# Keys, values, queries and energy of a one-core transformer block: four tiles from float32 operands, products paired on column halves

## The chip, the core and the metric

The kernel runs on one core of a Trainium2 chip. A core has a matrix engine (TensorE, PE in the profile, with its weight loads shown apart as PEld), VectorE (DVE), ScalarE (ACT), GpSimd (POOL) and SyncE (SP), each with its own instruction stream, and 16 DMA engines that move data between the chip's memory and the core's on-chip memory (SBUF). PE multiplies a stationary operand (the weights, up to 128 columns) with a moving operand and writes into eight accumulation banks (PSUM), which ACT and DVE read. The metric is the device time of one execution in microseconds (us).

## The reference

One attention layer without softmax, then a gated feed-forward network, each with a residual and a layer norm, for 4096 tokens of width 256. Cut to what matters here:

```python
Q = jnp.einsum('bne,de->bnd', x, wq)            # D = 64
K = jnp.einsum('bne,de->bnd', x, wk)
V = jnp.einsum('bne,de->bnd', x, wv)
energy = jnp.einsum('bnd,bne->bde', K, V)       # 64 x 64, over all tokens
context = jnp.einsum('bnd,bde->bne', Q, energy) * math.sqrt(3.0 / D)
out = jnp.einsum('bnd,ed->bne', context, wo)
x = _layernorm(x + out)
h = silu(x @ w1.T * w1_s) * (x @ w2.T * w2_s)   # 1024 wide, weights -1, 0, 1
h = gelu(h @ h1.T * h1_s)
h = gelu(h @ h2.T * h2_s)
x = _layernorm(x + h @ w3.T * w3_s)
```

All inputs and the output are float32.

## The kernel before

The tokens form eight tiles of 512 (T). A tile of the input comes in twice: transposed (`xt[t]`, 128 partitions x 2 x 512, for the attention's products) and as tokens (`x`, for the residual). Every engine runs its instructions in the order in which the program lists them; what one engine needs of another is kept by semaphores.

A product of float32 operands takes two records of load and multiply in the profile. The other way used here is the type float32r, in which a product is one record; an operand that it would round is split into two parts first: `hi`, the rounded value, cast by ACT, and `lo`, the rest, subtracted by DVE. Two products, with hi and with lo, are then added up.

**Attention, the stretch that the change touches (lines 421 to 694).** The transfers are listed on SP: `wkv` (keys' and values' weights), then `xt[0]` in two halves of its tokens, `xt[1]`, `wq1` (queries' weights, 64 columns), then `xt[2]` to `xt[7]` (lines 432 to 440); behind them blocks of a later layer's weights and `x`. On POOL: `wo`, `w1`, `w2` (from line 513), each after named transfers.

- `WARM` = 7 products of constants run on PE before any data is there (line 533).
- Tiles 0 to 2 (`WHOLE = 3`): `keys_values(t)` multiplies float32 tokens with `wkv`, 8 products of 128 columns into one bank, and ACT copies them to `kv[t]` (line 565).
- Tiles 3 to 7: `with_queries(t)` uses the two parts of the tokens (from `halves(t)`, lines 606 to 616) with the 192 columns `wvkq` of values, keys and queries: 16 products (line 578), two banks of two blocks of 128 tokens. ACT and DVE copy keys and values (lines 584 and 590), and the queries are split into hi and lo side by side in `stk[t]` (lines 585 and 586). `halves` is called two tiles ahead.
- Queries of tiles 0 to 2: `queries(t)`, four products of 512 columns with `wq`, in which the 64 columns stand twice (line 629); `stack(t)` makes the upper 64 partitions of `stk[t]` the rounded queries and the lower 64 the rest (lines 636 and 637).
- Queries of tiles 3 to 7 stand by tokens and are turned by PE: `turn_queries(t)`, four transposes (line 596), and `put_queries(t)`, a copy on ACT (line 600).
- `energy(t)` adds four products of 64 x 64 per tile to one 64-partition accumulator `pe` (line 619). ACT scales it into `es`, twice (line 663), one product with `wo` gives a 128 x 256 matrix (line 666), which ACT and DVE split into `m2hi` and `m2lo` (lines 667 and 668).
- `attention_out(t)` multiplies the stacked queries with both (lines 139 and 140). `attend_norm` adds the residual and normalizes on DVE, with a power on POOL (line 88).
- The first tile is turned (line 200), split (lines 208 and 209), and the feed-forward products begin: line 710 for the first half tile, then line 700.

`early` are sums of weight blocks on DVE for the later square layers (line 307 through `sums`), stored by POOL; `acc()` gives the six banks in turn.

**Behind it (from line 722)**: four passes of two tiles each through gate products (line 700), two square layers with seven block products each (line 295) and the last layer (line 855). In gaps of DVE, `check_job` compares weights with the rounded copies in use, piece by piece (23 pieces from `checks`, line 801); `inexact` holds the same for `wkv` (line 449). If anything differs, a general path runs afterwards.

The order of the main part, line 646 onwards:

```python
    for t in range(NT):
        if t < WHOLE:
            keys_values(t)
            continue
        if t + 2 < NT:
            halves(t + 2)
        elif t == NT - 1:
            early[0]()
        with_queries(t)
    queries(0)
    stack(0)
    halves(1)
    early[1]()
```

Of the kernel before, what the change touches and what calls it, by code (L numbers as in the profile page):

```python
# [32 lines left out]
KH = H // P  # L33
HK = KH // 2
EPS = 1e-5
WARM = 7
CSCALE = math.sqrt(3.0 / D)
SPREAD = 2.0**5
S1, S2, S3, S4, A11, A12, A22 = range(7)
# [5 lines left out]
def block_kernel(ctx: ExitStack, tc: tile.TileContext, a: dict, out: bass.AP):  # L45
# [19 lines left out]
    def const(name, shape, dt=F32):  # L65
        return cp.tile(shape, dt, tag=name, name=name)
# [9 lines left out]
    ones = const("ones", [P, 1])  # L76
    row = const("row", [1, P])
    eps = const("eps", [P, 1])
    inexact = const("inexact", [P, 1])
    m2hi = const("m2hi", [P, E], FR)  # L80
    m2lo = const("m2lo", [P, E], FR)
    flag = const("flag", [1, 1], I32)
# [23 lines left out]
    def weight(name, shape):  # L106
        return wp.tile(shape, FR, tag=name, name=name)
# [1 line left out]
    w1 = weight("w1", [P, KE, H])  # L109
    w2 = weight("w2", [P, KE, H])  # L110
    w3 = weight("w3", [P, KH, E])
    wq = weight("wq", [P, KE, P])
    stacks = weight("stk", [P, NT, T])
    stk = [stacks[:, t, :] for t in range(NT)]

# [17 lines left out]
    def attention_out(t):  # L133
        ps = []
        for g in range(NS // 2):
            po = aux[g].rearrange("p (j e) -> p j e", j=2)
            for j in range(2):
                q = stk[t][:, (2 * g + j) * P : (2 * g + j + 1) * P]
                nc.tensor.matmul(po[:, j, :], q, m2hi, start=True, stop=False)  # L139
                nc.tensor.matmul(po[:, j, :], q, m2lo, start=False, stop=True)  # L140
            ps.append(po)
        return ps

# [302 lines left out]

    nc.scalar.activation(once, mhalf[:, :1], AF.Silu)
    nc.scalar.copy(wvkq[:, :, : 2 * D], wkv)
    nc.vector.scalar_tensor_tensor(
        xT[:, 0, :, : 2 * D], wkv, 0.0, wvkq[:, :, : 2 * D].bitcast(F32),  # L450
        ALU.add, ALU.not_equal, accum_out=inexact,
    )

    def raw_blocks(layer, k, raw, queue=nc.sync):
        w = a[f"h{layer + 1}"]
# [67 lines left out]
    after(raw_blocks(0, 2, raws[2])[0], "w2")  # L523


    turn_of_acc = [5]

    def acc():
        turn_of_acc[0] += 1
        return bank[(turn_of_acc[0] - 1) % 6]  # L530
# [22 lines left out]
    def keys_values(t):  # L553
        x = xt[t]
        pk = acc().rearrange("p (s c) -> p s c", s=NS)
        for s in range(NS):
            for k in range(KE):
                nc.tensor.matmul(
                    pk[:, s, :], x[:, k, s * P : (s + 1) * P], wkv[:, k, :],
                    start=(k == 0), stop=(k == KE - 1),  # L560
                )
        kv_place(t)
        for i in ((0,), (2,), (3, 4))[t]:
            halves(i)
        nc.scalar.copy(kv[t], pk)

    def with_queries(t):

        kv_place(t)

        q = stk[t].rearrange("p (s i d) -> p s i d", s=NS, i=2)
        for g in range(2):
            ps = acc()[:, : 2 * V].rearrange("p (s c) -> p s c", s=2)
            for j in range(2):
                s = 2 * g + j
                for i, part in enumerate((xh[t], xl[t])):
                    for k in range(KE):
                        nc.tensor.matmul(  # L578
                            ps[:, j, :], part[:, k, s * P : (s + 1) * P], wvkq[:, k, :],
                            start=(i == 0 and k == 0), stop=(i == 1 and k == KE - 1),  # L580
                        )
# [23 lines left out]

    def halves(t):

        xh[t], xl[t] = places[t if t < 6 else t - 3]
        n = 2 if t in (WHOLE, WHOLE + 1) else 1
        for h in range(n):  # L610
            c = slice(h * T // n, (h + 1) * T // n)
            nc.scalar.copy(xh[t][:, :, c], xt[t][:, :, c])
            nc.vector.tensor_tensor(
                xl[t][:, :, c], xt[t][:, :, c], xh[t][:, :, c].bitcast(F32), ALU.subtract
            )

    def energy(t):
        for s in range(NS):
            nc.tensor.matmul(  # L619
                pe[:D], kv[t][:, s, :D], kv[t][:, s, D:P],  # L620
                start=(t == 0 and s == 0), stop=(t == NT - 1 and s == NS - 1),
            )

    def queries(t, ks=range(KE)):
        if t not in pq:
            pq[t] = acc()
        for k in ks:
            for i, part in enumerate((xh[t], xl[t])):
                nc.tensor.matmul(  # L629
                    pq[t], wq[:, k, :], part[:, k, :],  # L630
                    start=(k == 0 and i == 0), stop=(k == KE - 1 and i == 1),
                )

    def stack(t):

        nc.scalar.copy(stk[t], pq[t])
        nc.vector.tensor_tensor(  # L637
            stk[t][D:P], pq[t][D:P], stk[t][D:P].bitcast(F32), ALU.subtract
        )


    WHOLE = 3
    early = [*sums(0, 0, raws[0]), *sums(0, 1, raws[1])]
    for w in (wvkq[:, :, 2 * D :], wq[:, :, :D], wq[:, :, D:]):
        nc.vector.tensor_copy(w, wq1)
# [20 lines left out]
    nc.tensor.matmul(pm, es.rearrange("e c d -> e (c d)"), wo, start=True, stop=True)  # L666
    nc.scalar.copy(m2hi, pm)
    nc.vector.tensor_tensor(m2lo, pm, m2hi.bitcast(F32), ALU.subtract)
# [21 lines left out]
    split(0, 2)  # L690
    norm(2)
    norm(3)
    stack(1)
    stack(2)


    def gate_products(ps, w, o, slot, j, c=slice(0, T)):
# [87 lines left out]
    def second_sums(k):  # L785
# [167 lines left out]
    def bounds(step):  # L953

        if step == 0:
            nc.vector.tensor_reduce(some, mvo[:, : (NT - 2) * NS, 1], AX.X, ALU.max)
        if step == 1:
            nc.tensor.transpose(aux[0][:1, :P], some, ident)
            nc.vector.tensor_reduce(most[:1, 3:4], aux[0][:1, :P], AX.X, ALU.max)
        if step == 2:  # L960
            nc.tensor.matmul(aux[1][:, :1], row, most[:1, 3:4], start=True, stop=True)
            nc.vector.tensor_scalar(low, aux[1][:, :1], 1.0 / SPREAD, None, ALU.mult)
            nc.vector.tensor_scalar(high, aux[1][:, :1], SPREAD, None, ALU.mult)
        if step == 3:
            assert next_check.done == len(pieces) and not staged
            nc.vector.tensor_reduce(some, differ, AX.X, ALU.add)
            plus(some, some, inexact)
# [400 lines left out]
```

## Time and profile before

| what | value |
| --- | --- |
| median of 3 runs | 638.01 us (637.96 to 638.14) |
| the profiled execution's own time | 638.17 us |
| its span, first to last instruction | 636.4 us |
| last product of tiles 3 to 7 (L578) ends, queries of tile 0 (L629) begin | 22.11 us |
| energy (L619) begins | 23.15 us |
| first residual add (L160) begins | 29.94 us |
| first feed-forward product (L710) begins | 34.28 us |
| DMA rate 4.71 to 8.13 us, 8.13 to 12.39 us | 294 GB/s, 404 GB/s |
| landing of tiles 1, 2, 3, 4 of xt | 8.09, 10.26, 11.55, 12.83 us |

The profile is one execution. "Busy" is the time in which an engine has an instruction in flight; products on PE overlap, so the pace is read from start to start. An entry such as "[0.31 <-DMA f<-in_xt]" is idle time of the engine just before, and what ended it. In the view of waits the columns are: total us, times, longest us.

### The profile page before, as it was taken

The page shows a single profiled execution, that of the slowest core. Times are in us where ns is not written, and L with a number is a line of the kernel's source. Part 1 is how long each engine was busy: PE and PEld are TensorE (multiplying, and loading weights), DVE is VectorE, ACT ScalarE, POOL GpSimd, SP SyncE. Part 2 cuts the span into 40 slices and gives each one's busy share as a digit, 9 for nine tenths or more (in the row PEclk, how much of TensorE's full clock was granted, in tenths as well). Part 3 has the DMA queues.
Part 4 walks back from the last instruction along what each step waited for, and adds up shares of the span by engine and source line. Part 5 has one row for each costly group of instructions (what it writes and reads, how often), then busy time and mean ns, then how long its engine had stood idle before and what let it go on. Part 6 is the DMA issues. An engine that isn't in the chain of part 4 may idle for free.

```text
span 636.4 us, 9025 instructions
## 1 busy us (share of the span) xinstructions
PE 624.4 (98%) x3158; PEld 528.9 (83%) x3158; DVE 494.3 (78%) x776; ACT 381.0 (60%) x546; POOL 218.5 (34%) x280
## 2 busy tenths in 40 slices
PE   7999999999999999999999999999999999999995
PEld 5988888888898888888898888888898888888895
DVE  3899985889578788788667798798676896698456
ACT  5555462659845274655755457757764547765574
POOL 1233123204865409405545505603553700000043
PEclk9999999999999999999999999999999999999998
DMA  8899769977651167637851135645851035543201
GB/s 304 272 400 305 243 209 359 284 258 213 165 164 67 50 214 267 228 133 218 228 152 33 67 124 187 225 159 173 243 148 34 34 129 177 198 159 132 100 0 70
DMA packets 59681, 113.38 MB, mean 178 GB/s; under 512 B 19776, under 2 KB 34624, under 8 KB 59504
## 3 DMA queue, kind: packets, MB, share of 16 engines
q1 hardware_dynamic: 41424, 74.28, 35.4%
q0 software_dynamic: 18208, 38.48, 19.5%
q8 instruction: 26, 0.43, 0.3%
q14 instruction: 23, 0.19, 0.1%
HBM read 97.01 MB, written 18.87 MB: 182 GB/s over the span
## 4 chain that ended last, share of the span: by engine, by line
PE 95%; DVE 2%; DMA 1%; SPq 0%; issue 0%; ACT 0%; POOL 0%; DVEq 0%; POOLq 0%
PE bank L295 64%; PE bank L700 18%; PE bank L855 9%; PE bank L578 1%; DMA f<-in_xt 1%; PE bank L619 1%; PE bank L139 1%; PE bank L140 1%; DVE bn L147 0%; PE bank L629 0%; SPq L438 0%; DVE x L169 0%; POOL ra L88 0%; DVE stk L637 0%; PE bank L710 0%
## 5 line engine op out<-in xcount | busy, mean ns | idle before, releaser
L295 PE MATMUL bank<-hi,ws 128*128 128x512 f32 x896 | 348.7, 389 | 0.0
L295 PE MATMUL bank<-lo,ws 128*128 128x512 f32 x896 | 348.6, 389 | 0.0
L250 DVE TENSOR_TENSOR lo<-f,hi 128x1024 fp32r<-128x1024 f32 x142 | 168.4, 1224 | 58.0 <-ACT hi L249 57.4
L295 PEld LDWEIGHTS bank<-hi,ws 128*128 128x128 f32 x896 | 168.2, 188 | 34.9
L295 PEld LDWEIGHTS bank<-lo,ws 128*128 128x128 f32 x896 | 168.2, 188 | 34.9
L249 ACT CAST hi<-f 128x1024 fp32r<-128x1024 f32 x142 | 142.7, 1051 | 48.4 <-DVE f L307 24.7
L345 ACT ACTIVATE f<-f,hs 128x512 f32<-128x512 f32 x96 | 62.5, 715 | 68.6 <-DVE f L307 68.6
L700 PE MATMUL bank<-hi,w 128*128 128x512 f32 (+1 forms) x256 | 98.2, 386 | 0.0
L700 PE MATMUL bank<-lo,w 128*128 128x512 f32 (+1 forms) x256 | 98.1, 385 | 0.0
L719 ACT ACTIVATE f<-bank,s 128x512 f32<-128x512 f32 x64 | 44.0, 689 | 68.9 <-PE bank L700 65.6
L307 DVE TENSOR_TENSOR f<-f,f 128x1024 f32<-128x1024 f32 x64 | 76.5, 1221 | 4.5 <-ACT f L345 3.8
L307 DVE TENSOR_TENSOR f<-f,bank 128x512 f32<-128x512 f32 x96 | 61.5, 681 | 16.7 <-ACT f L400 12.8
L720 DVE SCALAR_TENSOR_TENSOR f<-bank,s,f 128x512 f32<-128x512 f32 x64 | 47.6, 748 | 25.2 <-PE bank L700 24.1
L855 PE MATMUL bank<-w,lo 128*128 128x256 f32 x240 | 57.9, 283 | 0.0
L855 PE MATMUL bank<-w,hi 128*128 128x256 f32 x240 | 57.9, 283 | 0.0
L700 PEld LDWEIGHTS bank<-hi,w 128*128 128x128 f32 x256 | 48.1, 188 | 9.4
L700 PEld LDWEIGHTS bank<-lo,w 128*128 128x128 f32 x256 | 48.1, 188 | 9.3
L234 POOL DMA_DIRECT2D xT<-x x96 | 52.2, 551 | 10.6 <-DVE x L923 4.4
L817 POOL DMA_DIRECT2D stage<-in_h x16 | 9.1, 569 | 110.6 <-DVE stage L843 105.7
L855 PEld LDWEIGHTS bank<-w,lo 128*128 128x128 f32 x240 | 46.1, 192 | 0.2
L855 PEld LDWEIGHTS bank<-w,hi 128*128 128x128 f32 x240 | 46.0, 192 | 0.2
L400 ACT COPY f<-bank 128x512 f32<-128x512 f32 x32 | 18.6, 587 | 29.8 <-PE bank L295 29.8
(168 smaller groups left out, 567.2 us busy)
## 6 DMA issues: line engine op xcount, KB each, us to landing
ws<-sw SPq DMA_DIRECT2D x100, 512.0 KB, 3.3
sw<-so POOLq DMA_DIRECT2D x16, 512.0 KB, 5.1
stage<-in_h POOLq DMA_DIRECT2D x16, 512.0 KB, 4.6
ws<-in_h POOLq DMA_DIRECT2D x12, 512.0 KB, 6.8
sw<-in_h SPq DMA_DIRECT2D x12, 512.0 KB, 5.0
x<-in_x SPq DMA_DIRECT2D x16, 256.0 KB, 5.5
f<-in_xt SPq DMA_DIRECT2D x7, 512.0 KB, 7.8
f<-in_h SPq DMA_DIRECT2D x6, 512.0 KB, 10.3
```

The lines of the kernel that those rows point to most:

```text
L234: moves.popleft()()
L249: nc.scalar.copy(hi[:, c, :], src[:, c, :])
L250: nc.vector.tensor_tensor(lo[:, c, :], src[:, c, :], hi[:, c, :].bitcast(F32), ALU.subtract)
L295: nc.tensor.matmul(ps[2 * h + o], w[:, k, o * P : (o + 1) * P], part[i][:, k, :], start=start and k == 0 and i == 0, stop=k == HK - 1 and ...
L307: engine.tensor_tensor(dst, u, v, op)
L345: nc.scalar.activation(dst, src, AF.Gelu, scale=sc[:, o : o + 1])
L400: nc.scalar.copy(bb[:, o], al[o])
L700: nc.tensor.matmul(ps[:, c], w[:, k, o * P : (o + 1) * P], part[:, 2 * j + k, c], start=(k == 0 and i == 0), stop=(k == KE - 1 and i == 1),)
L719: nc.scalar.activation(g, pa, AF.Silu, scale=s1[:, o : o + 1])
L720: nc.vector.scalar_tensor_tensor(g, pb, s2[:, o : o + 1], g, ALU.mult, ALU.mult)
L817: nc.gpsimd.dma_start(out=st[:, :n], in_=src.rearrange("p k o -> p (k o)")[:, c : c + n])
L855: nc.tensor.matmul(ps[:, :E], part[q][:, k, s * P : (s + 1) * P], w3[:, k0 + k, :], start=i % 2 == 0 and k == 0 and q == 0, stop=i % 2 == ...
```

## The change

- `WHOLE` is 4 in place of 3. Tiles 0 to 3 go through `keys_values`, whose products now run over the two halves of the width outside and the four token blocks inside; all four blocks of the bank are one accumulation group.
- `xt[0]` comes in two parts by width, not by tokens, and `wkv` between them; `wq1` comes after `xt[3]`. One warm-up product fewer.
- `with_queries` covers tiles 4 to 7. `halves` runs one tile ahead (tiles 4 and 5 before the products of tile 4, then tile t + 1). ACT copies keys and values of both groups, DVE none.
- The queries of tiles 0 to 3 come from float32 tokens and `wq1`, two tiles at a time (`two_queries`): tile t into partitions 0 to 63 of one bank and tile t + 1 into partitions 64 to 127, in four steps (two halves of the tokens x two halves of the width). `stack` puts odd tiles' rounded queries below and their rest above. The doubled weight `wq` is gone, and with it its check piece; `wq1` is tested once, as `wkv` is.
- The energy of even token blocks goes to partitions 0 to 63, that of odd blocks to 64 to 127; `es` has 128 rows, and `wo` stands twice below each other (a second transfer), so that the product with `wo` adds the two.
- `attention_out` does the products with `m2hi` of both blocks before those with `m2lo`.
- The order around the energy differs: `early[0]` follows the first queries, a step of the queries of tiles 2 and 3 stands between energy and `es`, the other three behind the transposes.

```diff
-WARM = 7
+WARM = 6
...
-            for j in range(2):
-                q = stk[t][:, (2 * g + j) * P : (2 * g + j + 1) * P]
-                nc.tensor.matmul(po[:, j, :], q, m2hi, start=True, stop=False)
-                nc.tensor.matmul(po[:, j, :], q, m2lo, start=False, stop=True)
+            for i, m in enumerate((m2hi, m2lo)):
+                for j in range(2):
+                    q = stk[t][:, (2 * g + j) * P : (2 * g + j + 1) * P]
+                    nc.tensor.matmul(
+                        po[:, j, :], q, m, start=(i == 0 and j == 0), stop=(i == 1 and j == 1),
+                        skip_group_check=True,
+                    )
...
-    wo = q1.tile([D, E], F32, tag="wo", name="wo")
-    es = q1.tile([D, 2, D], F32, tag="es", name="es")
+    wo = q1.tile([P, E], F32, tag="wo", name="wo")
+    es = q1.tile([P, 2, D], F32, tag="es", name="es")
+    WHOLE = 4
...
-    nc.sync.dma_start(out=wkv, in_=a["wkv"])
...
-    for t in range(NT):
-        for c in (slice(0, T // 2), slice(T // 2, T)) if t == 0 else (slice(0, T),):
-            last[t] = nc.sync.dma_start(out=xt[t][:, :, c], in_=a["xt"][t][:, :, c])
-        if t == 1:
+    for k in range(KE):
+        nc.sync.dma_start(out=xt[0][:, k, :], in_=a["xt"][0][:, k, :])
+        if k == 0:
+            nc.sync.dma_start(out=wkv, in_=a["wkv"])
+    for t in range(1, NT):
+        last[t] = nc.sync.dma_start(out=xt[t], in_=a["xt"][t])
+        if t == WHOLE - 1:
             nc.sync.dma_start(out=wq1, in_=a["wq"][:, :, :D])
...
+    def exact(i, src, c):
+        nc.vector.scalar_tensor_tensor(
+            xT[:, 0, :, c], src, 0.0, wvkq[:, :, c].bitcast(F32),
+            ALU.add, ALU.not_equal, accum_out=inexact[:, i : i + 1],
+        )
+    exact(0, wkv, slice(0, 2 * D))
+    nc.vector.tensor_copy(wvkq[:, :, 2 * D :], wq1)
+    exact(1, wq1, slice(2 * D, V))
...
-    after(nc.gpsimd.dma_start(out=wo, in_=a["wo"]), 5)
+    for j in range(2):
+        after(nc.gpsimd.dma_start(out=wo[j * D : (j + 1) * D], in_=a["wo"]), 5)
...
-        for s in range(NS):
-            for k in range(KE):
+        for k in range(KE):
+            for s in range(NS):
                 nc.tensor.matmul(
                     pk[:, s, :], x[:, k, s * P : (s + 1) * P], wkv[:, k, :],
-                    start=(k == 0), stop=(k == KE - 1),
+                    start=(k == 0 and s == 0), stop=(k == KE - 1 and s == NS - 1),
+                    skip_group_check=True,
                 )
         kv_place(t)
-        for i in ((0,), (2,), (3, 4))[t]:
-            halves(i)
         nc.scalar.copy(kv[t], pk)
...
-            if g == 0:
-                nc.scalar.copy(kv[t][:, c, :], ps[:, :, : 2 * D])
+            nc.scalar.copy(kv[t][:, c, :], ps[:, :, : 2 * D])
             nc.scalar.copy(q[:, c, 0, :], ps[:, :, 2 * D :])
...
-            if g == 1:
-                nc.vector.tensor_copy(kv[t][:, c, :], ps[:, :, : 2 * D])
...
-        xh[t], xl[t] = places[t if t < 6 else t - 3]
-        n = 2 if t in (WHOLE, WHOLE + 1) else 1
+        xh[t], xl[t] = places[t - WHOLE]
+        n = 2 if t == WHOLE else 1
...
         for s in range(NS):
+            h = slice(D * (s % 2), D * (s % 2 + 1))
             nc.tensor.matmul(
-                pe[:D], kv[t][:, s, :D], kv[t][:, s, D:P],
-                start=(t == 0 and s == 0), stop=(t == NT - 1 and s == NS - 1),
+                pe[h], kv[t][:, s, :D], kv[t][:, s, D:P],
+                start=(t == 0 and s < 2), stop=(t == NT - 1 and s >= NS - 2),
             )
-    def queries(t, ks=range(KE)):
...
+    def two_queries(t, steps=range(4)):
+        if t not in pq:
+            pq[t] = pq[t + 1] = acc()
+        for i in steps:
+            c, k = slice((i // 2) * T // 2, (i // 2 + 1) * T // 2), i % 2
+            for j in range(2):
                 nc.tensor.matmul(
-                    pq[t], wq[:, k, :], part[:, k, :],
-                    start=(k == 0 and i == 0), stop=(k == KE - 1 and i == 1),
+                    pq[t][j * D : (j + 1) * D, c], wq1[:, k, :], xt[t + j][:, k, c],
+                    start=(k == 0), stop=(k == KE - 1),
                 )
     def stack(t):
-        nc.scalar.copy(stk[t], pq[t])
-        nc.vector.tensor_tensor(
-            stk[t][D:P], pq[t][D:P], stk[t][D:P].bitcast(F32), ALU.subtract
-        )
+        up, down = (slice(0, D), slice(D, P))[:: 1 - 2 * (t % 2)]
+        nc.scalar.copy(stk[t][up], pq[t][up])
+        yield
+        nc.vector.tensor_tensor(stk[t][down], pq[t][up], stk[t][up].bitcast(F32), ALU.subtract)
+        yield
...
-        if t + 2 < NT:
-            halves(t + 2)
-        elif t == NT - 1:
-            early[0]()
+        if t == WHOLE:
+            halves(t)
+            halves(t + 1)
+        elif t + 1 < NT:
+            halves(t + 1)
         with_queries(t)
-    queries(0)
-    stack(0)
-    halves(1)
-    early[1]()
+    two_queries(0)
+    early[0]()
+    for _ in stack(0):
+        pass
+    stack1 = stack(1)
+    next(stack1)
     for t in range(NT):
         energy(t)
-    for j in range(2):
-        nc.scalar.mul(es[:, j, :], pe[:D, :], CSCALE)
-    turn_queries(3)
+    two_queries(2, [0])
+    nc.scalar.mul(es, pe.unsqueeze(1).to_broadcast([P, 2, D]), CSCALE)
+    early[1]()
...
-    queries(1)
-    put_queries(3)
+    next(stack1)
+    turn_queries(WHOLE)
     po = attention_out(0)
-    for t in range(4, NT):
+    put_queries(WHOLE)
+    for t in range(WHOLE + 1, NT):
         turn_queries(t)
         put_queries(t)
-    queries(2)
+    two_queries(2, range(1, 4))
...
-    checks = [(a["wq"], wq, KE * P)] + [
+    checks = [
```

More of the change, by code (lines that the diff above doesn't have):

```diff
@@ L78, in block_kernel @@
     eps = const("eps", [P, 1])
-    inexact = const("inexact", [P, 1])
+    inexact = const("inexact", [P, 2])
     m2hi = const("m2hi", [P, E], FR)
@@ L111, in block_kernel @@
     w3 = weight("w3", [P, KH, E])
-    wq = weight("wq", [P, KE, P])
     stacks = weight("stk", [P, NT, T])
@@ L448, in block_kernel @@
     nc.scalar.copy(wvkq[:, :, : 2 * D], wkv)
-    nc.vector.scalar_tensor_tensor(
-        xT[:, 0, :, : 2 * D], wkv, 0.0, wvkq[:, :, : 2 * D].bitcast(F32),
-        ALU.add, ALU.not_equal, accum_out=inexact,
-    )
+    def exact(i, src, c):
[6 more added lines that the diff above has]
+    exact(1, wq1, slice(2 * D, V))
     def raw_blocks(layer, k, raw, queue=nc.sync):
@@ L523, in block_kernel @@
     after(raw_blocks(0, 2, raws[2])[0], "w2")
-    turn_of_acc = [5]
+    turn_of_acc = [7]
     def acc():
@@ L618, in energy @@
         for s in range(NS):
+            h = slice(D * (s % 2), D * (s % 2 + 1))
             nc.tensor.matmul(
-                pe[:D], kv[t][:, s, :D], kv[t][:, s, D:P],
-                start=(t == 0 and s == 0), stop=(t == NT - 1 and s == NS - 1),
+                pe[h], kv[t][:, s, :D], kv[t][:, s, D:P],
+                start=(t == 0 and s < 2), stop=(t == NT - 1 and s >= NS - 2),
             )
-    def queries(t, ks=range(KE)):
+    def two_queries(t, steps=range(4)):
         if t not in pq:
-            pq[t] = acc()
-        for k in ks:
-            for i, part in enumerate((xh[t], xl[t])):
+            pq[t] = pq[t + 1] = acc()
+        for i in steps:
+            c, k = slice((i // 2) * T // 2, (i // 2 + 1) * T // 2), i % 2
+            for j in range(2):
                 nc.tensor.matmul(
-                    pq[t], wq[:, k, :], part[:, k, :],
-                    start=(k == 0 and i == 0), stop=(k == KE - 1 and i == 1),
+                    pq[t][j * D : (j + 1) * D, c], wq1[:, k, :], xt[t + j][:, k, c],
+                    start=(k == 0), stop=(k == KE - 1),
                 )
     def stack(t):
-        nc.scalar.copy(stk[t], pq[t])
-        nc.vector.tensor_tensor(
-            stk[t][D:P], pq[t][D:P], stk[t][D:P].bitcast(F32), ALU.subtract
-        )
-    WHOLE = 3
+        up, down = (slice(0, D), slice(D, P))[:: 1 - 2 * (t % 2)]
[3 more added lines that the diff above has]
+        yield
     early = [*sums(0, 0, raws[0]), *sums(0, 1, raws[1])]
-    for w in (wvkq[:, :, 2 * D :], wq[:, :, :D], wq[:, :, D:]):
-        nc.vector.tensor_copy(w, wq1)
     for t in range(NT):
@@ L692, in block_kernel @@
     norm(3)
-    stack(1)
-    stack(2)
+    for t in (2, 3):
+        for _ in stack(t):
+            pass
     def gate_products(ps, w, o, slot, j, c=slice(0, T)):
@@ L966, in bounds @@
             nc.vector.tensor_reduce(some, differ, AX.X, ALU.add)
-            plus(some, some, inexact)
+            for i in range(2):
+                plus(some, some, inexact[:, i : i + 1])
             nc.vector.tensor_scalar(fine, some, 0.0, None, ALU.is_le)
```

## The prediction

> **What bounds the kernel.** I read the page's busy shares and its chain first.
>
> ```profile
> PE 624.4 (98%) x3158; PEld 528.9 (83%) x3158; DVE 494.3 (78%) x776; ACT 381.0 (60%) x546; POOL 218.5 (34%) x280
> ...
> PE 95%; DVE 2%; DMA 1%; SPq 0%; issue 0%; ACT 0%; POOL 0%; DVEq 0%; POOLq 0%
> ```
>
> TensorE (PE) sets the end: it is busy for 98% of the span and makes 95% of the chain. Next, the view of PE's waits: everything it ever waited for.
>
> ```profile
> PE bank L1182 <- DVE most L1179: 3.1, 1, 3.1
> PE bank L558 <- DMA f<-in_xt: 2.2, 2, 1.4
> PE bank L534 <- PEq L1354: 0.9, 1, 0.9
> PE bank L578 <- DVE lo L613: 0.4, 1, 0.4
> PE bank L710 <- DVE stk L637: 0.3, 1, 0.3
> PE bank L710 <- ACT hi L208: 0.2, 1, 0.2
> ```
>
> L1182 is the final check, at the end. All other waits lie before 38 us; from there to 631 us PE waits for nothing. The change touches the time before 38 us, so its worth is by how much PE reaches L710 and L700 earlier or later. I walk that stretch in the timeline: PE and its weight loads (PEld), then ScalarE (ACT) and VectorE (DVE). The columns are start, length, instructions.
>
> ```profile
> 8.13 1.86 PEld L558 LDWEIGHTS bank<-wkv,f 128*128 128x128 f32 x16 [1.59 <-DMA f<-in_xt]
> 10.30 1.86 PEld L558 LDWEIGHTS bank<-wkv,f 128*128 128x128 f32 x16 [0.31 <-DMA f<-in_xt]
> ...
> 22.11 0.41 PE L629 MATMUL bank<-hi,wq 128*128 128x512 f32 x1
> 22.36 0.39 PE L629 MATMUL bank<-lo,wq 128*128 128x512 f32 x1
> ...
> 23.15 1.15 PE L619 MATMUL bank<-kv 128*64 128x64 f32 x16
> ...
> 25.01 1.95 PEld L619 LDWEIGHTS bank<-kv_so 128*64 128x64 f32 x32
> ...
> 27.61 0.70 PE L666 MATMUL bank<-wo,es 64*128 64x256 f32 x2
> ```
>
> ```profile
> 11.24 0.58 ACT L565 COPY kv<-bank 128x512 f32<-128x512 f32 x1
> 11.71 2.29 ACT L612 CAST hi<-f 128x512 fp32r<-128x512 f32 x4
> ...
> 15.90 1.08 ACT L612 CAST hi<-f 128x1024 fp32r<-128x1024 f32 x1
> ...
> 15.46 1.23 DVE L613 TENSOR_TENSOR lo<-f,hi 128x1024 fp32r<-128x1024 f32 x1 [0.46 <-ACT hi L612]
> ...
> 28.75 0.42 DVE L668 TENSOR_TENSOR m2lo<-bank,m2hi 128x256 fp32r<-128x256 f32 x1 [1.50 <-ACT m2hi L667]
> 29.94 0.75 DVE L160 TENSOR_TENSOR x<-x,bank 128x256 f32<-128x256 f32 x2 [0.77 <-PE bank L140]
> ```
>
> What to see: the loads of tiles 1 and 2 each wait for a transfer of xt, the copies and casts of ACT follow each other closely, and each DVE subtraction waits for its cast. A float32 product is two records, and the loads give their pace: L558 (1.86-0.19)/15 = 0.111 us each, so a tile of keys and values is 16 x 0.111 = 1.78; L619 (1.95-0.14)/31 = 0.058. L578 runs from its third pair at 13.55 to 22.11 us in 76 records: 0.113 each, 1.80 a tile. L629 (512 columns) repeats every 0.23.
>
> **The change, step by step.**
>
> *Loads.* The first product still needs wkv and 256 KB of tile 0: the same bytes, no gain. wq1 is now behind tile 3; it landed 0.22 us after tile 1 (8.31 against 8.09), so tile 2 comes at 10.26-0.22 = 10.04 and tile 3 at 11.33. One warm-up fewer: PE idles 0.83 us before L558, and if tile 0's products ran at half pace, they would take 3.6 us from 4.7 and end at 8.3 where tile 1 comes at 8.1; at most 0.2, and nothing taken. The second issue of wo (0.72 on POOL) falls into POOL's 5 us of waiting before w1; its 64 KB (0.16 us at 404 GB/s) push w1 to 24.5, which L710 needs at 34.3.
>
> *Tile 3 in float32.* PE starts tile 2 at 10.09 and, with tile 3 there, runs both: the copy of tile 3 on ACT starts at 10.09+1.78+2.02+0.04 = 13.93 (2.02 is the group of tile 0, whose copy came 0.04 later). Before, PE started L578 at 12.39 and ran from 13.25.
>
> *Tiles 4 to 7.* Now the new wait. In the program's order ACT splits tile 4 only after that copy, and halves run one tile ahead, not two: the cast of tile t+2 is queued behind the copies of tile t. Tile 4: 13.93 + 0.47 (copy to next cast, 11.24 to 11.71) + 0.62 + 0.03 + 0.69 + 0.04 (half a tile on ACT, then DVE) = 15.78, then 14 of 16 products x 0.113 = 1.58: end E4 = 17.36. Tile 5: its cast follows two half casts of 0.52, ends 16.5, DVE 1.25: E5 = 17.8+1.58 = 19.36. From E(t) to E(t+2): 0.2 to the last group's copy, 0.27 (kv copy, moved here from DVE), 0.17 (queries' copy), 1.05 (cast), 0.03, 1.22 (DVE), 0.04, 1.58 = 4.56 us, where PE needs 3.60. E6 = 21.92; E7 = 19.36+4.56 = 23.92. Before it was 22.11: **+1.8** although a tile of these products is gone.
>
> *Queries 0 and 1.* Removed: four products x 0.23 and their casts. Added: 16 records of 64 weight columns x 256. No row shows this form; two passes over 256 columns are the 512 columns of L629, so T = 0.23. One after the other: 3.68. Perfectly in pairs, but each product's second record behind its first: 9T = 2.07. [...] I take the middle, 2.27, plus 0.10 as PE lost before L619 (22.82+0.23 to 23.15): energy starts at 26.29.
>
> *Energy.* 64 records. Bounds: 3.87 as before (23.15 to 27.02) and half of it, 1.9. I take 2.0, near the half, because the rows give the 0.058 to the array's 64 columns alone (the 128-column form takes twice that), and other columns are free. End 28.29. [...]
>
> *To m2lo.* The es activation is one where two were; meanwhile PE runs step 0 of queries 2 and 3: 3T+0.1 = 0.8, so the wo product starts at 29.09 (es alone: 28.8). From it to m2lo's end is 1.56 (27.61 to 29.17): 30.65. The hi products of L139 now come first, so only lo waits: first pair of blocks out at 30.69+0.12+0.28 = 31.09. On DVE stack(1)'s subtraction (0.69) now stands between m2lo and the first add, which starts at 31.18, against 29.94: +1.24.
>
> *To L710.* From that add to the second normalized block is a chain on DVE and POOL, 3.50 us (29.94 to 33.44), unchanged: 34.68. PE in that time: second group 0.72 after lo, 31.41; 12 transposes x 0.109, 32.72; three steps of queries 2 and 3 at 0.52 + 0.25 + 0.1, 34.63; transposes at 34.73, the second at 34.9 where it was 33.49. PE is just the later: **+1.4 us**. Behind it the two stack subtractions (1.3 on DVE) stay two.
>
> *At nothing:* the second exactness test and wq1's cast (some 0.7 us on a DVE idle from 3.9 to 8.3); early sums, in DVE's gap before m2lo; one check piece fewer of 23 (0.4 us DVE) and all that follows moved by one call, hidden by PE, which waits for nothing after 38 us; uncovered it would gain 0.4.
>
> Sum: the profiled execution took 638.17 (636.4 span + 1.8 around it), 0.16 above the median 638.01. 638.0+1.4 = **639.4 us**.
>
> **Rivals.**
> 1. *The halves keep up* (not slower): no stall in tiles 5 to 7, E7 = 17.36+3x1.80 = 22.76, 1.16 earlier: 638.2; with the pairs perfect and tiles 1 to 3 half a us earlier (transfers ran at 294 GB/s before 8.1 us, 404 after), down to 636.6. It decides if the lo part of tile 6 is done before tile 5's products, a cycle under 3.6 us. For it: DVE loses its kv copies. Against: the ACT order in the code, and 1.05+1.22 in series.
> 2. *The energy gains nothing*, the queries do: loads of the two halves in one line. 3.87 for 2.0: 641.3. For it: the energy's pace equals the load's pace, 64 of 128 columns in half of 0.111. Against: the load is already beside the product.
> 3. *The halves don't run at the same time at all*, so that the change doesn't do what it says: 3.68 and 3.87, 0.92 and 2.76 for the rest: L710 about 5.5 later, 643.5. No row shows two products at once; none speaks against.
>
> **How the numbers follow.** Forecast 0.45 (its own range 638.4 to 640.3: the bounds of the pairs -0.6 and +0.6, landings 0.3), rival 1 0.22, rival 2 0.18, rival 3 0.15. A measurement tells 0.2%, 1.28 us, from none: 636.7 to 639.3. Slower: rivals 2 and 3, and the forecast's upper 0.26: 0.59. Same: its lower 0.19 and half of rival 1: 0.31. Faster: 0.10, rival 1's low end and what I overlooked. The range leaves out rival 3 and a little of rival 1: 637.0 to 641.6.
>
> **What would show it.** Right: a wait on lo before the products of tiles 4 to 7, together about 3 us; E7 near 23.9; energy in 2 us with records 0.03 apart; the first add near 31.2; no new wait after 40 us. Wrong: no lo wait after tile 4 (rival 1); L619 still 0.058 apart (rival 2); the 256-column records 0.23 apart (rival 3); or a wait beyond 40 us, which I exclude.

## The result and the profile after

The changed kernel takes 640.27 us at the median of six runs (639.20 to 641.53), against 638.04 for six runs of the kernel before beside it (637.96 to 638.30): a ratio of 1.0034, 95% interval 1.0021 to 1.0047. It is 2.2 us slower; the forecast was 1.4 us slower, 639.4, and the range 637.0 to 641.6 holds the result. The profiled execution is the fastest of the six, 639.20 us with a span of 637.3, where the one before had 638.17 and 636.4. So the trace below shows 0.9 us of the loss, and the other 1.3 have to come from what differs from run to run.

The waits of TensorE (columns: line and releaser, us in total, times, longest):

```profile
PE bank L574 <- DMA f<-in_xt: 1.3, 1, 1.3
PE bank L593 <- ACT hi L624: 1.2, 1, 1.2
PE bank L728 <- DVE stk L655: 0.9, 1, 0.9
...
PE bank L593 <- DVE lo L625: 0.9, 2, 0.6
```

L574 is `keys_values`, L593 `with_queries`, L728 the half products that were L710. The forecast's wait is there: before the products of tiles 4 to 7 TensorE now waits 1.2 us for a cast and 0.9 for the subtraction behind it, where it waited 0.4 in all. The wait for `stk` has grown from 0.3 to 0.9. The wait for tokens is one where there were two: the products of tiles 1, 2 and 3 now run without a pause.

The chain of work that ended last shows how these hang together (start, length, what):

```profile
2.21 5.34 DMA f<-in_xt
...
7.60 5.64 PE bank L574 x48
...
13.26 0.59 ACT kv_ws L580
13.85 0.53 ACT hi L624
...
14.39 0.70 DVE lo L625
...
36.26 0.69 DVE stk L655
36.97 0.59 ACT stk L653
...
37.59 0.70 DVE stk L655
```

First group of lines: the landing of tile 1 releases 48 products, their end releases the copy of tile 3 on ScalarE, and only behind that copy come tile 4's cast and VectorE's subtraction. As nothing in this chain has slack, a later landing of tile 1 moves everything behind it. Last group: VectorE's subtraction for tile 2, then ScalarE's copy for tile 3, then VectorE's subtraction for tile 3, strictly in turn.

The new products, in the timeline of TensorE (start, length, instructions):

```profile
23.52 1.95 PE L645 MATMUL bank<-f,wq 128*64 128x256 f32 x16
...
26.23 1.10 PE L633 MATMUL bank<-kv_so 128*64 128x64 f32 x32
```

The energy starts at 25.30, so the 16 records of the first queries take 1.78 us; single records start in pairs 6 or 7 ns apart, one pair every 0.216. The last 32 energy records take 0.94 (to 27.17): 0.029 each, half of the 0.058 before. Both kinds of products run in pairs on the two halves of the columns.

Step by step, with times in us in the profiled executions:

| | before | predicted | after | after less before |
|---|---|---|---|---|
| tile 7's products done, queries start | 22.11 | 23.92 | 23.52 | +1.41 |
| energy starts | 23.15 | 26.29 | 25.30 | +2.15 |
| energy done | 27.02 | 28.29 | 27.17 | +0.15 |
| wo product | 27.61 | 29.09 | 27.79 | +0.18 |
| first add of the residual | 29.94 | 31.18 | 30.11 | +0.17 |
| first half product (L710, L728) | 34.28 | 35.7 (+1.4) | 34.44 | +0.16 |
| third half product | 37.46 | 38.86 (+1.4) | 38.33 | +0.87 |
| first full product behind it (L700, L718) | 38.51 | | 39.27 | +0.76 |
| end of the span | 636.4 | 637.8 (+1.4) | 637.3 | +0.9 |

In this execution the late halves (+1.4) and the longer queries (+0.7) are paid back by the energy (-2.0) up to 0.16, and most of the loss of the span is made in one place, at the third half product, 38 us into the kernel. Its two times are not quite of the same record: in after the first of its eight records no longer waits and runs at 37.04, so 38.33 is the second, where 37.46 is the first. The first full product behind it compares like with like, and it is 0.76 later. From there to 632 us no wait of TensorE is over 0.15 us, so the 0.76 stays, and small pieces make it the 0.9 of the span.

### The profile page after: what moved, and what is told of

Read it like the earlier page. It is cut to its first block, busy times and chain, and to the rows that moved or that the text cites. A ratio compares the mean times of both kernels' runs of the same rounds, so it can differ in the third digit from the quotient of the medians.

```text
span 637.3 us, 9037 instructions
## 1 busy us (share of the span) xinstructions
PE 623.9 (98%) x3173; PEld 527.1 (83%) x3173; DVE 487.8 (77%) x764; ACT 378.8 (59%) x542; POOL 218.0 (34%) x280
## 4 chain that ended last, share of the span: by engine, by line
PE 95%; DVE 2%; DMA 1%; ACT 1%; issue 1%; POOL 0%; SPq 0%; POOLq 0%; DVEq 0%
PE bank L298 64%; PE bank L718 18%; PE bank L873 9%; PE bank L140 1%; PE bank L574 1%; PE bank L593 1%; DMA f<-in_xt 1%; PE bank L645 0%; DVE stk L655 0%; DVE lo L625 0%; DVE bn L150 0%; PE bank L633 0%; ACT hi L624 0%; POOL ra L88 0%; PE bank L728 0%
## 5 line engine op out<-in xcount | busy, mean ns | idle before, releaser
L718 PE MATMUL bank<-hi,w 128*128 128x512 f32 (+1 forms) x256 | 98.4, 386 | 0.0
L718 PE MATMUL bank<-lo,w 128*128 128x512 f32 (+1 forms) x256 | 98.1, 385 | 0.0
L718 PEld LDWEIGHTS bank<-hi,w 128*128 128x128 f32 x256 | 48.1, 188 | 9.8 <-DVE d L882 0.4
L718 PEld LDWEIGHTS bank<-lo,w 128*128 128x128 f32 x256 | 48.1, 188 | 9.3
```

Source lines behind the costliest of these rows:

```text
L718: nc.tensor.matmul(ps[:, c], w[:, k, o * P : (o + 1) * P], part[:, 2 * j + k, c], start=(k == 0 and i == 0), stop=(k == KE - 1 and i == 1),)
```

## Experiments

Three things were open: what makes the changed kernel's runs differ and their median 1 us worse than the profile; what the late halves and the shared bank each cost; and where the two microseconds of the energy go. Ratios are to the kernel before on the same chip (638.09, 637.96 and 638.03 us in the three sets).

| run | median us (runs) | ratio, 95% interval | tile 1 landed | third half product | full product, less before | span |
|---|---|---|---|---|---|---|
| before | 638.04 (6) | | 8.09 | 37.46 | | 636.4 |
| after | 640.27 (6) | 1.0034, 1.0021 to 1.0047 | 7.55 | 38.33 | +0.76 | 637.3 |
| e1_warm7 | 641.25 (8) | 1.0043, 1.0029 to 1.0057 | 8.43 | 39.21 | +1.63 | 638.2 |
| e2_warm11 | 640.32 (7) | 1.0036, 1.0022 to 1.0050 | 8.52 | 39.29 | +1.71 | 638.3 |
| e11_old_load_order | 640.95 (6) | 1.0049, 1.0035 to 1.0063 | 8.67 | 39.45 | +1.87 | 638.3 |
| e10_wq1_early | 640.36 (8) | 1.0033, 1.0020 to 1.0047 | 7.97 | 40.16 | +2.58 | 639.0 |
| e6_halves_ahead | 638.57 (12) | 1.0008, 0.9999 to 1.0017 | 8.55 | 36.26 | -1.32 | 636.1 |
| e3_copies_first | 640.65 (8) | 1.0036, 1.0017 to 1.0054 | 8.59 | 38.74 | +1.16 | 638.9 |
| e14_ahead_copies | 638.15 (12) | 0.9996, 0.9986 to 1.0006 | 8.70 | 37.40 | -0.18 | 637.0 |
| e4_energy_alone | 637.50 (12) | 0.9989, 0.9981 to 0.9998 | 8.00 | 35.84 | -1.62 | 635.7 |
| e8_all | 640.17 (6) | 1.0043, 1.0028 to 1.0059 | 8.49 | 35.57 | -2.01 | 637.9 |
| e9_energy_sums_later | 640.11 (6) | 1.0030, 1.0018 to 1.0042 | 8.44 | 35.56 | -1.89 | 638.1 |
| e12_sums_on_pool | 638.89 (11) | 1.0011, 1.0002 to 1.0020 | 6.79 | 34.03 | -3.54 | 636.7 |
| e13_energy_pool | 638.36 (11) | 1.0009, 0.9997 to 1.0021 | 8.02 | 35.66 | -1.80 | 636.3 |

The last four columns are of the profiled execution of each. The third half product is given by the first of its eight records that waits or follows the wait, which is the second in the kernels made from after; the next column is the start of the first full product behind it (L700 in before), less the 38.51 of before. It is read together with the span: where it is later than before, the span pays nearly all of it (after +0.76 and +0.9, e1 +1.63 and +1.8, e2 +1.71 and +1.9, e11 +1.87 and +1.9, e10 +2.58 and +2.6; e3 pays more, +1.16 and +2.5, in part by a later wait, shown below). Where it is earlier, little is gained or it is lost (e4 -1.62 and -0.7, e6 -1.32 and -0.3, e13 -1.80 and -0.1, e14 -0.18 and +0.6, e9 -1.89 and +1.7).

### The start: warm-up, landings, clock

**e1_warm7**, the changed kernel with the seventh warm-up product put back, and **e2_warm11**, with eleven:

```diff
-WARM = 6
+WARM = 7      # e2: 11
```

> The changed kernel with 7 warm-up products again. Theory A (the products of tile 0 now start at 3.8 us, before TensorE's full clock is granted at 4.9, and how long the half clock lasts differs from run to run): median 638.9 to 639.4, runs within 0.6 us of each other, tile 0's products at 0.111 us. Rival B (the spread of 639.2 to 641.5 comes from elsewhere, transfers for one): median 640.3 and the same spread of 2 us.

> The changed kernel with 11 warm-up products. Theory A: as with 7 or steadier, median 638.9 to 639.3, spread under 0.5 us; the later start of tile 0 (about 4.9 us) is hidden by the wait for tile 1 at 7.6. Rival B: median 640.3, spread 2 us. If warm-ups held up tile 0 and that set the end: over 640.5.

Neither gains: 641.25 and 640.32 against 640.27. The theory that the warm-up sets the loss falls. What their profiles show in its place is the rival: tile 1 landed 0.88 us later in e1 than in the profile of after, its products started at 8.47 in place of 7.60, and the third half product (+0.88) and the span (+0.9) moved with them, one for one. Nor did the seventh product bring the full pace sooner, as theory A had it: the float32 records come 0.21 us apart at first, and 0.111 apart from 4.95 us in after, 5.64 in e1 and 6.1 in e2.

**e11_old_load_order** puts the transfers of wkv and tile 0 back as they were (wq1 stays behind tile 3):

```diff
-    for k in range(KE):
-        nc.sync.dma_start(out=xt[0][:, k, :], in_=a["xt"][0][:, k, :])
-        if k == 0:
-            nc.sync.dma_start(out=wkv, in_=a["wkv"])
+    nc.sync.dma_start(out=wkv, in_=a["wkv"])
+    for c in (slice(0, T // 2), slice(T // 2, T)):
+        nc.sync.dma_start(out=xt[0][:, :, c], in_=a["xt"][0][:, :, c])
```

> The changed kernel with wkv first and tile 0 in two halves of its tokens, as before the change (wq1 stays behind tile 3). Theory (what differs between runs is when tile 1 lands, 7.55 to 8.6 us, and all behind it moves with it, since the products of tiles 1 to 3 run without a pause; the order of the first loads makes no difference): tile 1 between 7.6 and 8.6, median 640.0 to 640.6. Rival (the new order makes tile 1 late and unsteady): tile 1 at 8.0 in every profile, median 639.5, spread under 1 us.

640.95, not better than after, and tile 1 landed at 8.67. The order of tile 0's loads is not the cause. Over the fourteen profiles tile 1 lands between 6.79 and 8.70 us; what sets it within one kernel was not found.

**e10_wq1_early** moves wq1 back behind tile 1, to measure its price:

```diff
-        if t == WHOLE - 1:
+        if t == 1:
             nc.sync.dma_start(out=wq1, in_=a["wq"][:, :, :D])
```

> The changed kernel with the transfer of wq1 behind tile 1 again, as before the change. Theory (its 256-byte pieces delay tile 2 by 0.9 us, not the 0.22 that I took from its landing; but tile 2 is not what PE waits for any more, since tile 1 and its products last until then): tile 2 lands 1.7 to 2.2 us after tile 1 in place of 1.25, PE waits at most 0.5 for it, median 640.3 to 640.8. Rival: tile 2 lands 1.5 us after tile 1, no wait, 640.3.

Tile 2 landed 1.47 us after tile 1 (7.97, 9.44), and 1.25 in after (7.55, 8.80). By this pair wq1's 64 KB cost tile 2 0.2 us, as the forecast had it, not the 0.9 by which after and before differ in this step. But without wq1 there the step is 1.25 to 1.30 us in eight profiles and 1.51 in e12, so 0.2 is no more than what differs between executions. The median is that of after. But this profile shows something else. TensorE in the timeline:

```profile
14.83 0.47 PE L593 MATMUL bank<-wvkq,hi 128*128 128x192 f32 x2 [1.19 <-ACT hi L624]
15.56 0.47 PE L593 MATMUL bank<-wvkq,lo 128*128 128x192 f32 x2 [0.26 <-DVE lo L625]
...
16.76 0.39 PE L593 MATMUL bank<-wvkq,hi 128*128 128x192 f32 x2
...
17.73 0.63 PE L593 MATMUL bank<-wvkq,lo 128*128 128x192 f32 x2
...
20.62 0.39 PE L593 MATMUL bank<-wvkq,hi 128*128 128x192 f32 x2
```

From 17.09 to 20.51 us the granted clock is one half and the records come 0.214 us apart instead of 0.112; the mean clock of this run is 0.994, that of after's profile 0.997. This follows the two waits for the halves of tile 4, 1.45 us together. After, e1, e2, e3 and e11 have the same two waits, and their profiles have no such stretch: from tile 1's first product to the first queries they take 15.92 us, and e10 takes 17.34, so the stretch costs 1.42. Their other runs seem to have it, by the mean clock that each lists. In the 43 runs of these six kernels, 18 have a mean clock of 0.991 to 0.994, and 25 of 0.995 to 0.997; a stretch of 3.41 us at half pace lowers the mean by 3.41 x 0.5 / 637 = 0.003, about the step between them. The 18 average 641.5 us, the 25 640.0. None of the 72 runs of the kernel before beside the experiments shows a mean under 0.995. In after itself two of six are low, 641.1 against 639.8. Low means stand in other kernels too, though, without these waits: in 2 of 12 runs of e6, 1 of 12 of e14, 2 of 11 each of e12 and e13, 3 of 6 of e8 and 2 of 6 of e9, and in none of e4's 12. And the mean tells such runs only roughly: e14's profile, below, has a stretch of the same length, and its mean reads 0.995.

### The halves

**e6_halves_ahead** gives the halves their old lead: tiles 4 and 5 ahead of the copy of tile 3, then two tiles ahead.

```diff
         kv_place(t)
+        if t == WHOLE - 1:
+            halves(WHOLE)
+            halves(WHOLE + 1)
         nc.scalar.copy(kv[t], pk)
...
-        n = 2 if t == WHOLE else 1
+        n = 2 if t in (WHOLE, WHOLE + 1) else 1
...
-        if t == WHOLE:
-            halves(t)
-            halves(t + 1)
-        elif t + 1 < NT:
-            halves(t + 1)
+        if t + 2 < NT:
+            halves(t + 2)
```

> The changed kernel with the halves as the kernel before calls them: tiles 4 and 5 ahead of the copy of tile 3, then two tiles ahead. Theory (the changed kernel's loss is that lo and hi of tiles 4 to 7 come late: waits of 1.19, 0.26 and 0.61 us, and tile 7 ends at 23.5): no wait before L593 but some 0.2, tile 7 ends about 3 us earlier, the first add too; VectorE then waits for the second raw block (it lands at 36.5) some 0.5 us: median 637.9. Rival (the time is set by the landing of tile 1 and the transfers behind it, whatever the halves do): 639.5 or more.

638.57, and 1.7 of the 2.2 us are back. TensorE's timeline, in which no wait stands between the first line and the second:

```profile
8.59 5.62 PE L574 MATMUL bank<-wkv,f 128*128 128x128 f32 x48 [1.29 <-DMA f<-in_xt]
...
21.45 1.95 PE L648 MATMUL bank<-f,wq 128*64 128x256 f32 x16
```

From tile 1's first product to the first queries are 12.86 us; in after it is 23.52 - 7.60 = 15.92. The 3.06 us are the waits that are gone; the page counts 1.19, 0.26 and 0.61 from the modelled end of the product before, while from start to start of the records they cost 1.44, 0.50 and 0.78, and 0.26 more in two small pieces. That the median regains less has two grounds: this lead only brings the third half product to 36.26, and what is ahead of 37.46 pays little (below).

### The shared bank

**e3_copies_first** lets ScalarE copy both tiles before VectorE subtracts:

```diff
-    for t in (2, 3):
-        for _ in stack(t):
-            pass
+    both = [stack(t) for t in (2, 3)]
+    for _ in range(2):
+        for s in both:
+            next(s)
```

> The changed kernel with both ScalarE copies of stack(2) and stack(3) ahead of both VectorE subtractions. Theory: the second copy waits for the first subtraction because both read one bank, and that makes the third half product of L728 late by 0.65 us; the wait on stk before L728 falls from 0.94 to about 0.3 and the median by 0.65 to 639.6, with the spread of the changed kernel left. Rival: the subtractions are late because VectorE is busy before them: no change, 640.3.

VectorE's timeline has both subtractions together, where after has them at 36.26 and 37.59:

```profile
37.29 1.39 DVE L655 TENSOR_TENSOR stk<-bank,stk 64x512 fp32r<-64x512 f32 x2
```

TensorE's wait there falls from 0.94 to 0.30 us. The median shows nothing of it (640.65). In this profile tile 1 landed at 8.59, 1.04 later than in the profile of after, and a new wait of 0.5 us stands at 114.38 us, for sums that VectorE began late because a store landed late, at 110.98. By the starts of the products this wait costs 0.66. At their place the copies are worth what was expected: beside e2 and e11, whose tile 1 landed at 8.52 and 8.67, e3's third half product comes 0.55 and 0.71 us earlier. Their worth in the median is not settled: the wait at 114 us was seen in this execution only, while in e2, e10 and e11 the same store lands at 110.62 to 110.79 and TensorE doesn't wait.

**e14_ahead_copies** is e6 and e3 in one.

> The changed kernel with the halves ahead and the copies of stack(2) and stack(3) first, the sums unchanged. Theory (VectorE, waiting for the raw block from 36 to 37 us, sets what follows): the third half product of L728 comes 0.6 us earlier than with the halves ahead alone, but PE's wait for the turn of tile 1 near 46.6 grows by as much, and the median stays at 638.4 to 638.7. Rival: the 0.6 arrives, 638.0.

638.15, ratio 0.9996 with an interval across 1: the loss is undone. Against e6 it gains 0.4 us, where the wait alone was 0.63; the two intervals overlap, and the median lies between the theory's 638.4 and the rival's 638.0. Its profile can't decide between them, for another reason:

```profile
8.74 7.25 PE L574 MATMUL bank<-wkv,f 128*128 128x128 f32 x48 [1.75 <-DMA f<-in_xt]
```

These 48 products take 7.25 us, where in e6 they take 5.62: from 8.81 us, behind the wait for tile 1, the granted clock is one half for 3.41 us, though this kernel has no waits for the halves. Less the 1.63 us that this costs, the third half product would be at 35.77 in place of 37.40, ahead of e6's 36.26. All new products are in this kernel, in full pairs, and it is as fast as the kernel before, not faster.

### Where the energy's two microseconds go

**e4_energy_alone** is the kernel before with only the energy on two halves (and what it needs: wo twice, es on 128 partitions).

```diff
         for s in range(NS):
+            h = slice(D * (s % 2), D * (s % 2 + 1))
             nc.tensor.matmul(
-                pe[:D], kv[t][:, s, :D], kv[t][:, s, D:P],
-                start=(t == 0 and s == 0), stop=(t == NT - 1 and s == NS - 1),
+                pe[h], kv[t][:, s, :D], kv[t][:, s, D:P],
+                start=(t == 0 and s < 2), stop=(t == NT - 1 and s >= NS - 2),
             )
```

> The kernel before with the energy alone on two halves of the columns (wo twice, es of 128 rows; two transfers for wo). Theory: energy takes 1.85 us in place of 3.87, the chain from es to the first add moves up by 2.0, and nothing gives it back: 636.1. Rival: the wait for m2lo or for the first weights or x takes part of it back: 637 to 638.

637.50, ratio 0.9989 (0.9981 to 0.9998): the fastest kernel of the study, 0.6 us under before at the median, and not the 2 that the energy saves. The third half product comes 1.62 us earlier, at 35.84. VectorE's timeline just behind it:

```profile
37.59 0.69 DVE L307 TENSOR_TENSOR so<-f 128x512 fp32r<-128x512 f32 x1 [1.02 <-DMA f<-in_h]
```

The sums of the next raw weight block wait 1.02 us for the block, which lands at 37.49. In the kernel before they began at 38.11 and found it landed (37.60). The block doesn't come earlier because TensorE does. And what VectorE loses there it can't make up, as the windows of before and of e4 show (window, length, then busy us and instructions of PE, PEld, DVE, ACT and POOL, clock, DMA share and GB/s), one line of each:

```profile
48.00:61.00 13.00, 13.00 (x66) 10.83 (x65) 12.96 (x18) 7.57 (x11) 4.63 (x7) 1.00 1.13 299
```

```profile
48.00:61.00 13.00, 13.00 (x64) 10.89 (x63) 12.93 (x18) 7.04 (x10) 4.00 (x6) 1.00 1.13 305
```

From 48 to 61 us VectorE is busy for 12.96 of 13 us in the kernel before: it is full beside a full TensorE. An earlier TensorE meets a VectorE that isn't earlier by as much, and e4 waits 0.26 us for a normalized tile at 46.59:

```profile
46.59 1.80 PE L200 MATMUL bank<-ident,x 128*128 128x128 f32 x8 [0.26 <-DVE x L169]
```

These eight transposes of tile 1 are where the gain goes. They start at 46.59 where before started them at 47.80, and their starts are spread over 1.53 us where before took 0.95. Ahead of them e4 leads before by 1.62 us, behind them by 0.63. The same place takes e6's lead from 1.32 to 0.52, e13's from 1.80 to 0.37 and e12's from 3.54 to 1.14, and it turns e14's 0.18 into a lag of 0.26.

**e9_energy_sums_later** (e4) and **e8_all** (e6 with e3's copies) move these sums behind the normalization of tile 1, to keep VectorE free before:

```diff
             split(2, 4)
-            early[2]()
-            early[3]()
...
                 norm(s)
+            early[2]()
+            early[3]()
```

> The kernel before with the energy on two halves and the same two sums behind the normalization of tile 1. Theory (in the run with the energy alone 1.6 us arrived at L711 and 1.0 of it was lost where the sums waited for the raw block): no wait of VectorE for in_h near 37 us, no wait of PE near 46.6, median 636.4. Rival: the same 637.5, lost to another wait in the same stretch.

> As the one with the halves ahead, and both copies of stack(2) and stack(3) first, and the sums of the second raw block (early 2 and 3) behind the normalization of tile 1. Theory: a further 0.65 from the copies and the wait for the raw block gone: 636.8, under the kernel before. Rival: VectorE, full between 42 and 61 us, now holds up the gates or the turn of tile 1: 637.9 or more with a new wait of PE between 44 and 60 us.

Both are slower, 640.11 and 640.17. The waits of TensorE in e9:

```profile
PE bank L701 <- DVE lo L209: 2.0, 1, 2.0
...
PE bank L701 <- DVE f L721: 0.8, 1, 0.8
```

They lie at 53.0 and 64.96 us, where before had none, and e8 has the same two (2.01 and 0.75). The sums have been moved to where VectorE has even less room.

**e12_sums_on_pool** (e6 with e3's copies) and **e13_energy_pool** (e4) give the four sums of that block to GpSimd instead:

```diff
-    early = [*sums(0, 0, raws[0]), *sums(0, 1, raws[1])]
+    early = [*sums(0, 0, raws[0]), *sums(0, 1, raws[1], nc.gpsimd)]
```

> The changed kernel with the halves ahead, the copies of stack(2) and stack(3) first, and the four sums of the second raw block on GpSimd in place of VectorE (their place in the program unchanged). Theory (from 37 us on VectorE is what sets the pace: it waits for the raw block and is then full until 61 us; without the sums PE keeps the 2 us that it is ahead): no wait of PE from 36 to 110 us, median 636.5, under the kernel before. Rival (GpSimd, slower per element, now holds up the powers of tile 1 behind the sums, or slows VectorE): a wait of PE on x L172 near 47 us of 1 us or more, 638 or more.

> The kernel before with the energy on two halves and the four sums on GpSimd. Theory: the 1.0 us that the run with the energy alone lost at 46.6 stays won: 636.6. Rival: as above, 637.5 or more.

638.89 and 638.36, at the median worse than the same kernels without it (638.15, 637.50), though the intervals of the ratios touch. A sum takes 1.30 us on GpSimd and 0.69 on VectorE, and in e12 the powers of the normalization (L88, on GpSimd too) start behind them, at 44.32. TensorE's waits in e12:

```profile
PE bank L203 <- DVE x L172: 1.7, 3, 1.1
```

In e12 the first full product comes 3.5 us earlier than before, in part by an early landing of tile 1 (6.79), and all of it is gone by 51 us: 1.15 + 0.40 us of waits for normalized tiles at 45.56 and 46.61, then 3.4 us at half clock, with records of 512 columns 0.43 us apart up to 50.5 us and 0.23 apart from 50.9.

## Why the prediction came out as it did

**The sign and the mechanism were right.** The casts of tile t+2 are queued behind the copies of tile t, a lead of one tile doesn't cover cast and subtraction in series, and TensorE waits before tiles 4 and 6. From the copy of tile 3 to the end of tile 7 the forecast had 23.92 - 13.93 = 9.99 us, and 23.52 - 13.26 = 10.26 were measured to the first query. E6 shows the cause: with the old lead the waits are gone, and 1.7 of the 2.2 us.

**The landings.** Tile 3's copy came 0.67 earlier than forecast in the profile of after, since tile 1 landed early. In e1 it landed at 8.43 and the first add came at 30.98, 0.2 from the forecast's 31.18. The forecast took one landing where there is a spread of nearly 2 us, and gave it 0.3 in its range. It also had TensorE wait for tile 2, at 10.04; in after tile 2 landed at 8.80, before the products of tile 1 were done, and only tile 1's landing counts.

**The pairs were taken too dear.** Queries 1.78 for 2.27 and the switch of 0.10; energy 1.87 for 2.0. Together 0.7 us. Even the lower bound of the queries, 2.07, was too high: it took 0.23 a record and set one half a record behind the other (9T), and the pairs come every 0.216 with both halves starting 6 or 7 ns apart. The 0.20 that its 2.27 has above that bound, for weight loads left uncovered between the records, was the author's estimate, and no run shows it: the 16 records took 1.78 in all. Rivals 2 and 3 are refuted by the same rows and by the energy's 0.029 a record.

**The step that failed** is "Behind it the two stack subtractions (1.3 on DVE) stay two", costed at nothing. They stay two, but tiles 2 and 3 now share one bank, and ScalarE's copy of tile 3 is released by VectorE's subtraction of tile 2. That puts 0.65 us (36.97 to 37.59 on ScalarE) between the two subtractions: a wait of 0.94 for 0.33 before. E3 takes it away, 0.30. Less these 0.64 us, the first full product of after would have come at 38.63, 0.1 behind before and not 0.8.

**The clock was left out.** The forecast priced the waits by their length. In 18 of 43 runs with these waits the mean clock was 0.003 lower, and the time 1.4 us longer. That a stretch at half clock does this is shown in e10's profile, where it costs 1.42 us; that it is the same stretch in the other runs is inferred from their mean clock. It doesn't need these waits: e14's profile has it behind the wait for tile 1, for 1.63 us.

**Rival 1**, that the halves keep up (638.2), did not happen in the changed kernel, and its time is what e14 measures when they are made to, 638.15, but by other steps: e14 has the bank's wait removed too, and its pairs are faster than this rival's. What then eats a lead has its place behind 38 us, at the transposes of tile 1, where e4 loses 0.99 us, e6 0.80 and e14 0.44. The view of TensorE's waits in before shows none there, and the forecast read from it that a microsecond won before 38 us is won at the end. It did not look at how much room VectorE has from 38 to 61. In e4 0.6 us came of 2.

So it is by luck that the net is near the forecast. Errors cancel: too dear pairs (-0.7) against the bank (+0.65), and clock and landings on top. **Open** stay: what sets the landing of tile 1, what e3's 0.6 us are worth in the median, and what decides whether a run has the stretch at half clock. Of the 0.6 us by which e14's span is longer than that of before, 0.26 is there behind the transposes; the rest was not followed.

## What to carry to other kernels

When a stage of casts and subtractions feeds a matmul engine, its lead must cover the whole series (copy ahead in the queue, cast, subtraction), not only the throughput of each engine; count what stands ahead of the cast in program order. Here a lead of one tile left waits of 1.19, 0.26 and 0.61 us, and a lead of two left none. Two products on the two halves of the columns paid in full here (a record of the energy every 0.029 us for every 0.058), but two tiles that then share a bank also share their readers, which put 0.65 us between two subtractions: put the first engine's reads of both ahead of the second engine's. And before a gain at a full engine is booked, look at the windows behind it for a second engine that is also full, and at the transfers that both wait for: here losses of 0.76 to 2.58 us passed straight to the end, and of the 1.62 us that e4 gained the span kept 0.7.

## What was not expected of the hardware

- Float32 records on the two column halves ran side by side: in after the two of a pair start 6 or 7 ns apart, 256-column records every 0.216 us a pair, 64-column ones every 0.058. For 64 columns that is the pace that one half alone had (0.058 in before); no run has the 256-column form on one half alone.
- Waits of 1.19 and 0.26 us in e10, and of 1.15 and 0.40 in e12, with products between, were followed by 3.41 us at half clock, though not in every run. In e14 a single wait of 1.75 us was. The profiles of after, e1, e2, e3 and e11 have the same waits of 1.19 and 0.26 us and no such stretch.
- The pace at the start differs between executions: float32 records come 0.21 us apart at first, and 0.111 apart from 4.2 us (e8) to 10.3 us (e4), in no order of the number of warm-up products, while the profile's clock reads 1.00 (e4, 4.77 to 10.27 us).
- Tile 1, behind the same bytes, landed between 6.79 and 8.70 us.
